# Layer 2's norm statistics and first chunk moved beside layer 1's gathers

## The chip, the core and the metric

The kernel runs on one core of a Trainium2 chip. Its engines are named as in the profile: PE (TensorE: matmuls, with PEld for its weight loads), DVE (VectorE), ACT (ScalarE), POOL (GpSimd) and SP (SyncE, here used only to issue DMA). Each engine works through its own queue in order and waits on semaphores where it needs another engine or a transfer. The metric is the device time of one execution in microseconds; the median of three runs is 15601.95 us.

## What is computed

The reference is a four-layer network on `x` of 2 x 64 x 64 x 128 (two batches of 4096 tokens with 128 channels). Cut to what matters here:

```python
# layer 1: deformable 3x3 convolution; each of 9 taps reads 4 neighbours at computed places
x = x + _L1_conv_ref(_gn(x), ...)
# layer 2, first half: norm over the channels of each token, then a selective scan
t = _to_tokens(x)
t = t + _L2_attn_ref(_ln_t(t), W_in, W_delta, W_B, W_C, W_out, A, D)

def _ln_t(v, eps=1e-5):
    return (v - mean(v, -1)) / sqrt(var(v, -1) + eps)

def _L2_attn_ref(x, ...):
    xs, z = split(x @ W_in, 2)             # 256 channels each
    delta, Bv, Cv = xs @ W_delta, xs @ W_B, xs @ W_C
    # state[d, n] = exp(delta[d] * A[d, n]) * state + delta[d] * Bv[n] * xs[d], token after token
    # y[d] = sum over n of state[d, n] * Cv[n];  out = (y * silu(z)) @ W_out
```

Layer 0 is another selective scan, layer 2's second half a spectral convolution, layer 3 a linear attention and a mixture of experts. None of these is changed.

## The kernel before

`X` holds all 8192 tokens as 64 tiles of 128 tokens by 128 channels in on-chip memory (32 KB a partition) through layers 0 and 1.

**Layer 1** (`layer1`). After some preparation it runs a loop over the 64 tiles, 32 of batch 0 and then 32 of batch 1. For a tile, POOL issues nine indirect gathers from a table in DRAM (line 598), which fill a buffer `G` of 18 KB a partition; there are four such buffers. DVE multiplies `G` by the weights of the neighbours (line 605, an operation of 4608 elements a partition). PE sums and transposes the result into `pv` (line 612), ACT copies it to `vt` (line 613), PE multiplies it by the kernel of the convolution into `po` (line 616), and DVE adds `po` to `X` (line 617). At tile 36 of the program's text stands `mix`, which prepares weights for layer 2's second half with many small DVE operations, some of ACT, and transfers on SP's queue.

**The seam.** `norm_tokens` then takes bn_stats and bn_aggr of all 64 tiles (lines 629 and 630) and computes from them `rs` (one over the standard deviation, by `rsqrt`, lines 81 to 87) and `sh` (minus mean times `rs`, line 632). `move` writes `X` to `x1` in DRAM in eight transfers (line 1410).

**Layer 2** (`layer2`) works on 16 chunks of 512 tokens. Before a chunk's scan its `prologue` is run: it reads the chunk from `x1` (line 779), normalises and transposes it (786, 787), multiplies by `w_in` (797) and, with weights that it loads one after the other (806), by `w_delta`, `w_b` and `w_c` (813, 822). What comes out is `ea` (816, 818), `drow` in DRAM (828), `g` (830) and `cv` (832). Prologues of later chunks run in steps beside the scan of the chunk before them; the first has nothing beside it, and its steps follow each other:

```python
            for _ in prologue(*todo[0], got):
                pass
            ready[0] = got.pop()
            for r in range(2):
                load_row(r)
            make_inputs(0)
```

In the scan, `load_row` (line 1127, on SP's queue) broadcasts four rows of `drow` to all partitions, `make_inputs` lets POOL multiply them by `g` into `S` (line 1139), ACT computes the decays `dA` from the row and `a_t` (line 1193), and DVE scans (line 1195). `ea` enters only from the second chunk of a batch on, `cv` only in the contraction after a group's scan.

**What sets the order.** Outside layer 2's scan the framework orders the instructions of each engine by a simulated run and places the semaphores; on the chip each engine then keeps that order. In layer 2's scan the order of the text is kept (`manual_schedule`). Pools of memory are stacked: those of layer 2 lie over those of layers 0 and 1 and over `X`, so a first write into them waits until what lay there has been read for the last time.

Of the kernel before, what the change touches and what calls it, by code (L numbers as in the profile page):

```python
# [16 lines left out]
F32 = mybir.dt.float32  # L17
# [8 lines left out]
P = 128  # L26
B, HH, WW, C = 2, 64, 64, 128
L = HH * WW
# [458 lines left out]
        nc.gpsimd.dma_start(out=dst, in_=z[: TS - 3, :])  # L487


def layer1(k, table, mix):  # L490


    tc, nc, ins, X = k.tc, k.nc, k.ins, k.X
    with ExitStack() as es:
# [97 lines left out]
        for t in range(NT):  # L592
            b, i = divmod(t, NTB)
            if t == NTB + 4 and mix is not None:
                mix(es)
            G = gp.tile([P, 9, 4 * C], F32, name="G")
            for o in range(9):
                nc.gpsimd.indirect_dma_start(  # L598
                    out=G[:, o, :],
                    out_offset=None,  # L600
                    in_=table[b],
                    in_offset=bass.IndirectOffsetOnAxis(ap=idxs[b][:, i * 9 + o : i * 9 + o + 1], axis=0),
                )
            V = G.rearrange("p o (q c) -> p (o q) c", c=C)
            nc.vector.tensor_tensor(V, V, wts[b][:, i * 9 : (i + 1) * 9, :].rearrange("p o q -> p (o q)").unsqueeze(2).to_broadcast([P, 36, C]), ALU.mult)  # L605

            vt = wk.tile([P, 9 * P], F32, name="vt")
            for g, n in ((0, 4), (4, 4), (8, 1)):
                pv = gs.tile([P, N], F32, name="pv1")
                for o in range(n):  # L610
                    for q in range(4):
                        nc.tensor.matmul(pv[:, o * P : (o + 1) * P], V[:, (g + o) * 4 + q, :], k.ident, start=q == 0, stop=q == 3)
                nc.scalar.copy(vt[:, g * P : (g + n) * P], pv[:, : n * P])  # L613
            po = po_.tile([P, C], F32, name="po2")
            for o in range(9):
                nc.tensor.matmul(po, vt[:, o * P : (o + 1) * P], w_k[:, o, :], start=o == 0, stop=o == 8)
            nc.vector.tensor_tensor(X[:, t, :], po, X[:, t, :], ALU.add)

def norm_tokens(k, rs, sh):

    tc, nc, X = k.tc, k.nc, k.X
    with tc.tile_pool(name="l2n", bufs=1) as pre:
        st = pre.tile([P, NT, 6], F32, name="st6")
        mv = pre.tile([P, NT, 2], F32, name="mv2")
        for i in range(NT):
            nc.vector.bn_stats(st[:, i, :], X[:, i, :])
            nc.vector.bn_aggr(mv[:, i, :], st[:, i, :])  # L630
        rsqrt(nc, pre, rs, mv[:, :, 1], 1e-5, [P, NT], "ln2")
        nc.vector.scalar_tensor_tensor(sh, mv[:, :, 0], -1.0, rs, ALU.mult, ALU.mult)

# [77 lines left out]
    return (wdr, mdr), work  # L714


def layer2(k, x1, x3, rs, sh, wdr, mdr):

# [18 lines left out]
    with ExitStack() as es:  # L739
# [34 lines left out]
            return x[t0 : t0 + T, :].rearrange("(i p) c -> p i c", p=P)  # L774

        def prologue(b, c, got):

            xi = sm.tile([P, NB, C], F32, name="xi", tag="s2")
            nc.sync.dma_start(out=xi, in_=chunk(x1, b, c))
            for _ in range(4):  # L780
                yield
            pt = ps.tile([P, N], F32, name="pt", tag="ps")
            for j in range(NB):
                i = b * NTB + c * NB + j
                o = sm.tile([P, C], F32, name="xn", bufs=2)
                nc.scalar.activation(o, xi[:, j, :], AF.Identity, bias=sh[:, i : i + 1], scale=rs[:, i : i + 1])
                nc.tensor.transpose(pt[:, j * P : (j + 1) * P], o, k.ident)
                yield
            xt = sm.tile([P, T], F32, name="xt2", tag="s2")
            nc.scalar.copy(xt, pt)  # L790
            xtd = ddr.tile([P, T], F32, name="xtd")
            nc.sync.dma_start(out=xtd, in_=xt)
            yield
            xs = sm.tile([P, 2, N], F32, name="xs", tag="s4")
            for h in range(2):
                px = ps.tile([P, N], F32, name="px2", tag="ps")
                nc.tensor.matmul(px, w_in[:, h * P : (h + 1) * P], xt, start=True, stop=True)
                yield
                nc.scalar.copy(xs[:, h, :], px)
            ea = cst.tile([P, 2, 256], F32, name="ea")  # L800
            g = gc.tile([P, 2, T], F32, name="g")
            cv = gc.tile([P, 2, T], F32, name="cv")
            drow = ddr.tile([256, T], F32, name="drow")
            for w_, what in (("w_delta2", 0), ("w_b2", 1), ("w_c2", 2)):
                w = cst.tile([P, 2, 256], F32, name="w")
                nc.sync.dma_start(out=w, in_=ins[w_].rearrange("(a p) c -> p a c", p=P))
                yield
                yield
                if what == 0:

                    pd = ps.tile([P, N], F32, name="pd0", tag="ps")
                    for i in range(2):
                        nc.tensor.matmul(pd[:, :256], xs[:, i, 0:1].to_broadcast([P, P]), w[:, i, :], start=i == 0, stop=i == 1)
                    yield
                    yield
                    nc.vector.tensor_tensor(ea, a_t, pd[:, :256].unsqueeze(1).to_broadcast([P, 2, 256]), ALU.mult)
                    yield
                    nc.scalar.activation(ea, ea, AF.Exp)
                for h in range(2):
                    pw = ps.tile([P, N], F32, name="pw2", tag="ps")  # L820
                    for i in range(2):
                        nc.tensor.matmul(pw, w[:, i, h * P : (h + 1) * P], xs[:, i, :], start=i == 0, stop=i == 1)  # L822
                    yield
                    yield
                    if what == 0:
                        d = sm.tile([P, N], F32, name="d", tag="s2")
                        nc.scalar.copy(d, pw)
                        nc.sync.dma_start(out=drow[h * P : (h + 1) * P, :], in_=d)
                    elif what == 1:
                        nc.vector.tensor_tensor(g[:, h, :], pw, xs[:, h, :], ALU.mult)  # L830
                    else:
                        nc.scalar.copy(cv[:, h, :], pw)
            got.append((xtd, g, cv, drow, ea))

        def epilogue(b, c, xtd, zd):

# [330 lines left out]

        with tc.manual_schedule():
            got = []
            for _ in prologue(*todo[0], got):  # L1170
                pass
            ready[0] = got.pop()
            for r in range(2):
                load_row(r)
            make_inputs(0)
# [237 lines left out]
def kernel(tc, ins, out, stages=STAGES):  # L1413
    nc = tc.nc
    with ExitStack() as es:
        pool = es.enter_context(tc.tile_pool(name="top", bufs=1))
        dr = es.enter_context(tc.tile_pool(name="topd", bufs=1, space=DRAM))
        k = Ctx(tc, ins, pool)
        x = ins["x"]
        two = "2a" in stages or "2f" in stages  # L1420
        if two:
            rs = pool.tile([P, NT], F32, name="rs2")
            sh = pool.tile([P, NT], F32, name="sh2")
        if two or "0" in stages or "1" in stages:
            with tc.tile_pool(name="x01", bufs=1) as xp:
                k.X = xp.tile([P, NT, C], F32, name="X")
                move(nc, k.X, tokens(x))
                if "1" in stages:
                    table = [dr.tile([TS * TS, 4 * C], F32, name=f"table{b}") for b in range(B)]
                    with tc.tile_pool(name="zt", bufs=1) as zp:  # L1430
                        zero_table(k, zp, table)
                mix = None
                if two:
                    weights, mix = mixing_weights(k, dr)
                if "0" in stages:
                    layer0(k)
                if "1" in stages:
                    layer1(k, table, mix)
                elif two:
                    with ExitStack() as e2:  # L1440
                        mix(e2)
                if two:
                    norm_tokens(k, rs, sh)
                x = dr.tile([B * L, C], F32, name="x1")
                move(nc, tokens(x), k.X)
        if two:
            x3 = dr.tile([B * L, C], F32, name="x3")
            layer2(k, x, x3, rs, sh, *weights)
            x = x3
        with tc.tile_pool(name="x3", bufs=1) as xp:  # L1450
            k.X = xp.tile([P, NT, C], F32, name="X")
            move(nc, k.X, tokens(x))
            if "3a" in stages:
                layer3a(k)
            if "3f" in stages:
                layer3f(k, out)
            else:
                move(nc, tokens(out), k.X)
# [106 lines left out]
```

## Time and profile before

| | us |
|---|---|
| median of 3 runs | 15601.95 |
| lowest and highest run | 15600.6, 15609.41 |
| the profiled execution's own time | 15611.47 |
| its span, first to last instruction | 15609.7 |
| first gather of layer 1 to last (line 598) | 4330.1 to 5315.2 |
| last X add of layer 1 ends (line 617) | 5338.67 |
| first S of layer 2 begins on POOL (line 1139) | 5391.72 |

Busy shares of the span are DVE 88%, POOL 86%, PE 76%, ACT 63%. Times in the profile are microseconds from the start of the span. The page lists groups of instructions as: line, engine, operation, output and inputs, count, then busy time and mean duration in ns, then the idle time of the engine before them and what ended most of it. In a timeline each row is: start, length, engine, line, operation, and in brackets the idle time before it and what released it. The chain of waits goes from the end of a window back: at each step to what released it.

### The profile page before, as it was taken

The numbers are of one execution on the slowest core, as the hardware profiler recorded it, in microseconds if no ns is written. First come the engines' busy times: TensorE is split into PE (matmuls) and PEld (weight loads), VectorE is DVE, ScalarE is ACT, GpSimd is POOL, SyncE is SP. The second block draws the span as 40 slices with busy tenths as digits, with TensorE's granted clock in tenths as the row PEclk, the third lists the DMA queues.
The fourth block names the chain that finished last, engine by engine and source line by source line (L and its number), as shares of the span: only waits on it lengthen the run. The fifth ranks groups of instructions, "written<-read, shape, count | busy, mean of one in ns | idle before, by whom it ended". The sixth has DMA issues, their size and how long they took to land.

```text
span 15609.7 us, 191436 instructions
## 1 busy us (share of the span) xinstructions
PE 11894.2 (76%) x69838; PEld 7117.6 (46%) x69838; DVE 13768.3 (88%) x12194; ACT 9829.7 (63%) x15891; POOL 13474.0 (86%) x5144
## 2 busy tenths in 40 slices
PE   6666676666677645486976978979788899898897
PEld 2222232222367512154653645646445555555565
DVE  7999979999853499999999999999999999999964
ACT  5666646666410177777777777777777777777752
POOL 6888848888578699999999999999999999999960
PEclk9999999999988767697987989989999999999998
DMA  2111111211175445465655556656666666666643
GB/s 82 71 71 70 67 60 71 73 68 71 63 226 160 137 151 163 154 195 177 204 188 169 195 179 194 202 182 200 194 193 195 192 197 202 192 196 199 188 160 130
DMA packets 1211438, 2373.47 MB, mean 152 GB/s; under 512 B 346744, under 2 KB 923896, under 8 KB 1044352
## 3 DMA queue, kind: packets, MB, share of 16 engines
q1 hardware_dynamic: 1163072, 2206.74, 43.2%
q0 software_dynamic: 46560, 153.18, 3.3%
q8 instruction: 552, 9.04, 0.2%
q14 instruction: 390, 3.19, 0.1%
q10 hardware_dynamic: 864, 1.32, 0.0%
HBM read 2018.49 MB, written 342.41 MB: 151 GB/s over the span
## 4 chain that ended last, share of the span: by engine, by line
POOL 35%; PE 14%; DVE 11%; DMA 3%; ACT 2%; issue 2%; SPq 0%; POOLq 0%; ACTq 0%; DVEq 0%
POOL S L1139 34%; DVE S L1195 10%; PE pef L1023 7%; PE Z L1157 2%; PE acc L996 2%; DMA row<-drow 2%; PE pw L822 1%; POOL S L1145 1%; ACT dA L1193 1%; ACT ze L1163 1%; DMA w<-in_w_b_dram 0%; PE acc L1058 0%; DMA e<-mdr 0%; ACT e L1003 0%; DMA w<-in_w_c_dram 0%
## 5 line engine op out<-in xcount | busy, mean ns | idle before, releaser
L1195 DVE TENSOR_TENSOR_SCAN S<-dA,S 128x512 f32<-128x512 f32 x8192 | 9226.4, 1200 | 397.2 <-ACT dA L1193 208.2
L1139 POOL TENSOR_TENSOR S<-row,g 128x4096 f32<-128x4096 f32 x1024 | 9102.2, 8895 | 280.6 <-DMA row<-drow 232.4
L1193 ACT ACTIVATE dA<-row,a_t 128x512 f32<-128x512 f32 x8192 | 5616.2, 692 | 2158.3 <-DVE S L1195 2123.3
L1157 PE MATMUL Z<-S,cv 128*32 128x256 f32 x32768 | 2504.9, 436 | 1486.0 <-ACT ze L1163 1227.3
L1023 PE MATMUL pef<-hk,ur 128*128 128x256 f32 x14336 | 3507.0, 388 | 137.8 <-ACT e L1003 122.0
L1023 PEld LDWEIGHTS pef<-hk,ur 128*128 128x128 f32 x14336 | 2642.0, 191 | 1076.6 <-issue 562.1
L376 POOL TENSOR_TENSOR S<-du,br 128x1024 f32<-128x1024 f32 x1024 | 2409.7, 2356 | 282.7 <-DVE M L401 164.9
L387 DVE TENSOR_TENSOR_SCAN S<-dA,S 128x1024 f32<-128x1024 f32 x1024 | 2338.0, 2283 | 161.2 <-ACT dA L385 101.9
L1157 PEld LDWEIGHTS Z<-S,cv 128*32 128x32 f32 x32768 | 1002.0, 121 | 2695.7 <-issue 1286.1
L419 PE MATMUL yp<-M,ident 128*128 128x512 f32 x4096 | 1974.5, 604 | 2.9 <-DVE M L401 2.9
L419 PEld LDWEIGHTS yp<-M,ident 128*128 128x128 f32 x4096 | 789.9, 193 | 2147.7 <-issue 2112.7
L385 ACT ACTIVATE dA<-dt,an 128x511 f32<-128x511 f32 x2048 | 1406.5, 687 | 194.2 <-DVE S L387 148.1
L401 DVE TENSOR_TENSOR M<-S,pcn 128x1024 f32<-128x1024 f32 x1024 | 1250.4, 1221 | 151.9 <-PE pcn L343 51.9
L343 PE MATMUL pcn<-cs,sel 80*128 80x512 bf16 x1024 | 394.7, 385 | 1183.6 <-DVE M L401 1174.7
L1163 ACT COPY ze<-Z 128x512 f32<-128x512 f32 x1024 | 1123.0, 1097 | 236.9 <-PE Z L1157 204.6
L996 PE MATMUL acc<-e,mw 128*128 128x512 f32 x1920 | 1047.6, 634 | 31.2 <-ACT e L1003 30.5
L598 POOL DMA_INDIRECT G<-table,idx x576 | 810.8, 1408 | 202.6 <-issue 170.3
L1023 PEld LDWEIGHTS pef<-hd,ur 128*128 128x128 f32 x4096 | 758.2, 194 | 491.5 <-issue 236.0
L1023 PE MATMUL pef<-hd,ur 128*128 128x256 f32 (+1 forms) x4096 | 877.8, 341 | 101.6 <-ACT e L1003 95.3
L389 ACT COPY stt<-S 128x2 f32<-128x2 f32 x896 | 169.3, 189 | 1067.9 <-DVE S L387 1064.8
L605 DVE TENSOR_TENSOR G<-G,wt 128x4608 f32<-128x4608 f32 x64 | 317.6, 4963 | 579.6 <-DMA G<-table,idx 486.4
L613 ACT COPY vt<-pv 128x512 f32<-128x512 f32 (+1 forms) x192 | 88.4, 480 | 864.9 <-remote 598.0
(331 smaller groups left out, 8503.8 us busy)
## 6 DMA issues: line engine op xcount, KB each, us to landing
row<-drow SPq DMA_DIRECT2D x1024, 1024.0 KB
br<-bc SPq DMA_DIRECT2D x256, 1024.0 KB
zd<-ze SPq DMA_DIRECT2D x1024, 256.0 KB
hk<-in_phi_dram SPq DMA_DIRECT2D x128, 576.5 KB
hk<-in_phi_dram SPq DMA_DIRECT2D x96, 704.5 KB
hd<-in_phi_dram SPq DMA_DIRECT2D x512, 128.5 KB
mw<-wdr SPq DMA_DIRECT2D x480, 128.0 KB
hk<-in_phi_dram SPq DMA_DIRECT2D x160, 320.5 KB
```

The costliest lines, as they stand in the source:

```text
L376: nc.gpsimd.tensor_tensor(S, du, br[:, n % 4, :].unsqueeze(1).to_broadcast([P, 2, T]), ALU.mult)
L385: nc.scalar.activation(dA[:, h, rest], dt[:, h, rest], AF.Exp, scale=an[:, kk * 2 + h, n : n + 1])
L387: nc.vector.tensor_tensor_scan(flat, dflat, flat, 0.0, ALU.mult, ALU.add)
L401: nc.vector.tensor_tensor(M, S, pcn.unsqueeze(1).to_broadcast([P, 2, T]), ALU.mult)
L419: nc.tensor.matmul(yp[:, h, :], k.ident, M[:, h, :], start=False, stop=n == 15)
L996: nc.tensor.matmul(acc.rearrange("p a s -> p (a s)"), ms[f][:, o, :], e, start=box["first"], stop="whole" in box and (f, o) == todo[-1])
L1023: nc.tensor.matmul(pe[:, a, 256 - n :], ur[:, par, j, :], h[:, at : at + n], start=i == 0, stop=i + 1 == len(mm))
L1139: nc.gpsimd.tensor_tensor(S, row.unsqueeze(1).to_broadcast([P, 2, R, T]), g.unsqueeze(2).to_broadcast([P, 2, R, T]), ALU.mult)
L1157: nc.tensor.matmul(Z[32 * j : 32 * j + 32, q], cv[:, h, s], S[:, h, :, s], start=h == 0, stop=h == 1)
L1163: nc.scalar.copy(ze.rearrange("p q t e -> p q e t"), Z)
L1193: nc.scalar.activation(dA, row[:, j % R, :], AF.Exp, scale=a_t[:, h, d : d + 1])
L1195: nc.vector.tensor_tensor_scan(s, dA, s, 0.0, ALU.mult, ALU.add)
```

## The change

`norm_tokens` becomes a maker of a function `each(t)`, which layer 1 calls after the X add of tile t: bn_stats and bn_aggr of this tile, after every fourth tile a transfer of four tiles to `x1`, and after the last tile of a batch the `rsqrt` and `sh` of that batch. Its small tiles lie in the pool of `X`. The body of `prologue` becomes a function `scan_inputs`, word for word. At tile 40 of the text (`t == NTB + 8`), `first_inputs` runs it for chunk 0 in layer 1, with its own loads of half of `w_in` and of `a_t`, in a pool of its own and with layer 1's PSUM tiles, and writes `g`, `cv` and `ea` to DRAM. Layer 2 reads these three back by transfers on ACT's queue where it ran the first prologue.

```diff
@@ layer1
             if t == NTB + 4 and mix is not None:
                 mix(es)
+            if t == NTB + 8 and first is not None:
+                first(es, ps)
...
             nc.vector.tensor_tensor(X[:, t, :], po, X[:, t, :], ALU.add)
+            if each is not None:
+                each(t)

-def norm_tokens(k, rs, sh):
-    tc, nc, X = k.tc, k.nc, k.X
-    with tc.tile_pool(name="l2n", bufs=1) as pre:
...
-        for i in range(NT):
-            nc.vector.bn_stats(st[:, i, :], X[:, i, :])
-            nc.vector.bn_aggr(mv[:, i, :], st[:, i, :])
-        rsqrt(nc, pre, rs, mv[:, :, 1], 1e-5, [P, NT], "ln2")
-        nc.vector.scalar_tensor_tensor(sh, mv[:, :, 0], -1.0, rs, ALU.mult, ALU.mult)
+def norm_tokens(k, pool, x1, rs, sh):
...
+    def each(t):
+        nc.vector.bn_stats(st[:, t, :], X[:, t, :])
+        nc.vector.bn_aggr(mv[:, t, :], st[:, t, :])
+        if t % 4 == 3:
+            nc.sync.dma_start(out=out[:, t - 3 : t + 1, :], in_=X[:, t - 3 : t + 1, :])
+        if t % NTB == NTB - 1:
+            b = slice(t + 1 - NTB, t + 1)
+            rsqrt(nc, pool, rs[:, b], mv[:, b, 1], 1e-5, [P, NTB], "ln2")
+            nc.vector.scalar_tensor_tensor(sh[:, b], mv[:, b, 0], -1.0, rs[:, b], ALU.mult, ALU.mult)
+    return each

+def first_inputs(k, es, ps, dr, x1, rs, sh):
+    nc = k.nc
+    pool = es.enter_context(k.tc.tile_pool(name="l2e", bufs=1))
+    w_in = pool.tile([P, 256], F32, name="w_in0")
+    nc.sync.dma_start(out=w_in, in_=k.ins["w_in2"][:, :256])
+    a_t = pool.tile([P, 2, 256], F32, name="a_t0")
+    nc.sync.dma_start(out=a_t, in_=k.ins["a2"].rearrange("(a p) c -> p a c", p=P))
+    got = []
+    for _ in scan_inputs(k, 0, 0, x1, rs, sh, w_in, a_t, pool, pool, pool, dr, ps, got):
+        pass
+    xtd, g, cv, drow, ea = got[0]
+    kept = []
+    for t, name in ((g, "g0"), (cv, "cv0"), (ea, "ea0")):
+        d = dr.tile(list(t.shape), F32, name=name)
+        nc.sync.dma_start(out=d, in_=t)
+        kept.append(d)
+    return xtd, kept[0], kept[1], drow, kept[2]

@@ layer2
             got = []
-            for _ in prologue(*todo[0], got):
-                pass
-            ready[0] = got.pop()
+            xtd, g0, cv0, drow, ea0 = early
+            g, cv, ea = gc.tile([P, 2, T], F32, name="g"), gc.tile([P, 2, T], F32, name="cv"), cst.tile([P, 2, 256], F32, name="ea")
+            for dst, src in ((g, g0), (cv, cv0), (ea, ea0)):
+                nc.scalar.dma_start(out=dst, in_=src)
+            ready[0] = xtd, g, cv, drow, ea
             for r in range(2):
                 load_row(r)
             make_inputs(0)

@@ tile_hybrid_kernel
-                    layer1(k, table, mix)
+                    x1, early = dr.tile([B * L, C], F32, name="x1"), []
+                    each = norm_tokens(k, xp, x1, rs, sh)
+                    first = lambda es, ps: early.append(first_inputs(k, es, ps, dr, x1, rs, sh))
+                    layer1(k, table, mix, each, first)
...
-                    norm_tokens(k, rs, sh)
-                x = dr.tile([B * L, C], F32, name="x1")
-                move(nc, tokens(x), k.X)
...
-            layer2(k, x, x3, rs, sh, *weights)
+            layer2(k, x, x3, rs, sh, *weights, early[0])
```

More of the change, by code (lines that the diff above doesn't have):

```diff
@@ L487, in zero_table, with layer1 @@
         nc.gpsimd.dma_start(out=dst, in_=z[: TS - 3, :])
-def layer1(k, table, mix):
+def layer1(k, table, mix, each, first):
     tc, nc, ins, X = k.tc, k.nc, k.ins, k.X
@@ L617, in layer1 @@
             nc.vector.tensor_tensor(X[:, t, :], po, X[:, t, :], ALU.add)
-def norm_tokens(k, rs, sh):
-    tc, nc, X = k.tc, k.nc, k.X
-    with tc.tile_pool(name="l2n", bufs=1) as pre:
-        st = pre.tile([P, NT, 6], F32, name="st6")
-        mv = pre.tile([P, NT, 2], F32, name="mv2")
-        for i in range(NT):
-            nc.vector.bn_stats(st[:, i, :], X[:, i, :])
-            nc.vector.bn_aggr(mv[:, i, :], st[:, i, :])
-        rsqrt(nc, pre, rs, mv[:, :, 1], 1e-5, [P, NT], "ln2")
-        nc.vector.scalar_tensor_tensor(sh, mv[:, :, 0], -1.0, rs, ALU.mult, ALU.mult)
+            if each is not None:
+                each(t)
+def norm_tokens(k, pool, x1, rs, sh):
+    nc, X = k.nc, k.X
+    st = pool.tile([P, NT, 6], F32, name="st6")
+    mv = pool.tile([P, NT, 2], F32, name="mv2")
+    out = x1.rearrange("(i p) c -> p i c", p=P)
+    def each(t):
[8 more added lines that the diff above has]
+    return each
 DW = 257
@@ L714, in mixing_weights, with scan_inputs @@
     return (wdr, mdr), work
-def layer2(k, x1, x3, rs, sh, wdr, mdr):
+def scan_inputs(k, b, c, x1, rs, sh, w_in, a_t, sm, cst, gc, ddr, ps, got):
+    nc, ins, T = k.nc, k.ins, N
+    NB = T // P
+    xi = sm.tile([P, NB, C], F32, name="xi", tag="s2")
+    nc.sync.dma_start(out=xi, in_=x1[b * L + c * T : b * L + (c + 1) * T, :].rearrange("(i p) c -> p i c", p=P))
+    for _ in range(4):
+        yield
+    pt = ps.tile([P, N], F32, name="pt", tag="ps")
+    for j in range(NB):
+        i = b * NTB + c * NB + j
+        o = sm.tile([P, C], F32, name="xn", bufs=2)
+        nc.scalar.activation(o, xi[:, j, :], AF.Identity, bias=sh[:, i : i + 1], scale=rs[:, i : i + 1])
+        nc.tensor.transpose(pt[:, j * P : (j + 1) * P], o, k.ident)
+        yield
+    xt = sm.tile([P, T], F32, name="xt2", tag="s2")
+    nc.scalar.copy(xt, pt)
+    xtd = ddr.tile([P, T], F32, name="xtd")
+    nc.sync.dma_start(out=xtd, in_=xt)
+    yield
+    xs = sm.tile([P, 2, N], F32, name="xs", tag="s4")
+    for h in range(2):
+        px = ps.tile([P, N], F32, name="px2", tag="ps")
+        nc.tensor.matmul(px, w_in[:, h * P : (h + 1) * P], xt, start=True, stop=True)
+        yield
+        nc.scalar.copy(xs[:, h, :], px)
+    ea = cst.tile([P, 2, 256], F32, name="ea")
+    g = gc.tile([P, 2, T], F32, name="g")
+    cv = gc.tile([P, 2, T], F32, name="cv")
+    drow = ddr.tile([256, T], F32, name="drow")
+    for w_, what in (("w_delta2", 0), ("w_b2", 1), ("w_c2", 2)):
+        w = cst.tile([P, 2, 256], F32, name="w")
+        nc.sync.dma_start(out=w, in_=ins[w_].rearrange("(a p) c -> p a c", p=P))
+        yield
+        yield
+        if what == 0:
+            pd = ps.tile([P, N], F32, name="pd0", tag="ps")
+            for i in range(2):
+                nc.tensor.matmul(pd[:, :256], xs[:, i, 0:1].to_broadcast([P, P]), w[:, i, :], start=i == 0, stop=i == 1)
+            yield
+            yield
+            nc.vector.tensor_tensor(ea, a_t, pd[:, :256].unsqueeze(1).to_broadcast([P, 2, 256]), ALU.mult)
+            yield
+            nc.scalar.activation(ea, ea, AF.Exp)
+        for h in range(2):
+            pw = ps.tile([P, N], F32, name="pw2", tag="ps")
+            for i in range(2):
+                nc.tensor.matmul(pw, w[:, i, h * P : (h + 1) * P], xs[:, i, :], start=i == 0, stop=i == 1)
+            yield
+            yield
+            if what == 0:
+                d = sm.tile([P, N], F32, name="d", tag="s2")
+                nc.scalar.copy(d, pw)
+                nc.sync.dma_start(out=drow[h * P : (h + 1) * P, :], in_=d)
+            elif what == 1:
+                nc.vector.tensor_tensor(g[:, h, :], pw, xs[:, h, :], ALU.mult)
+            else:
+                nc.scalar.copy(cv[:, h, :], pw)
+    got.append((xtd, g, cv, drow, ea))
@@ L731, in layer2 @@
+def layer2(k, x1, x3, rs, sh, wdr, mdr, early):
     tc, nc, ins = k.tc, k.nc, k.ins
@@ L776, in prologue @@
         def prologue(b, c, got):
[L778 to L832, printed above, removed]
@@ L833, in prologue @@
-            got.append((xtd, g, cv, drow, ea))
+            return scan_inputs(k, b, c, x1, rs, sh, w_in, a_t, sm, cst, gc, ddr, ps, got)
         def epilogue(b, c, xtd, zd):
@@ L1436 @@
                     layer0(k)
+                each = first = None
+                if two:
+                    x1, early = dr.tile([B * L, C], F32, name="x1"), []
+                    each = norm_tokens(k, xp, x1, rs, sh)
+                    first = lambda es, ps: early.append(first_inputs(k, es, ps, dr, x1, rs, sh))
                 if "1" in stages:
-                    layer1(k, table, mix)
+                    layer1(k, table, mix, each, first)
                 elif two:
@@ L1441 @@
                         mix(e2)
+                        for t in range(NT):
+                            each(t)
+                        first(e2, e2.enter_context(tc.tile_pool(name="l2ep", bufs=2, space=PSUM)))
                 if two:
-                    norm_tokens(k, rs, sh)
-                x = dr.tile([B * L, C], F32, name="x1")
-                move(nc, tokens(x), k.X)
+                    x = x1
+                else:
+                    x = dr.tile([B * L, C], F32, name="x1")
+                    move(nc, tokens(x), k.X)
         if two:
             x3 = dr.tile([B * L, C], F32, name="x3")
-            layer2(k, x, x3, rs, sh, *weights)
+            layer2(k, x, x3, rs, sh, *weights, early[0])
             x = x3
```

## The prediction

> **What bounds the kernel now.** I read the page first, then the chain of waits around the seam between layers 1 and 2, then the timelines of POOL, DVE, ACT and SP inside layer 1's gather loop. The scan of layer 2, two thirds of the span, keeps POOL and DVE near 90% busy, and the change leaves its code alone. What it touches is the seam, and the loop into which the seam's work goes. The chain of waits from 5290 to 5420 us (start, length, what):
>
> ```profile
> 5315.19 3.67 DMA G<-table,idx
> 5319.17 4.96 DVE G L605
> ...
> 5338.38 0.29 DVE X L617
> 5338.67 0.39 DVE st L629 x2
> ...
> 5355.33 0.21 DVE ln_v L81
> ...
> 5357.50 0.23 DVE sh L632
> 5357.76 0.50 ACT xn L786
> ...
> 5386.22 4.90 DMA row<-drow
> 5391.72 8.82 POOL S L1139
> 5400.57 7.58 DVE S L1195 x7
> ```
>
> Layer 1 ends with the last X add at 5338.67. POOL's first S, which starts the scan, begins at 5391.72, so the seam is 53.05 us long and serial: 64 pairs of statistics (to 5355.33, 16.7), the rsqrt and shift (to 5357.76, 2.4), the first chunk's preparation (to 5386.22, 28.5) and the row broadcast (5.5).
>
> The loop is bound by POOL. The page:
>
> ```profile
> L598 POOL DMA_INDIRECT G<-table,idx x576 | 810.8, 1408 | 202.6 <-issue 170.3
> ```
>
> 810.8 busy plus 170.3 of issue fills 981 of the 986 us from 4330 to 5315: the next gather is always ready to go. The timelines of POOL and DVE for one tile:
>
> ```profile
> 4695.29 4.96 DVE L605 TENSOR_TENSOR G<-G,wt 128x4608 f32<-128x4608 f32 x1 [9.94 <-DMA G<-table,idx]
> 4700.16 0.28 DVE L617 TENSOR_TENSOR X<-po,X 128x128 f32<-128x128 f32 x1
> ```
> ```profile
> 4695.01 0.95 POOL L598 DMA_INDIRECT G<-table,idx  x1 [0.30 <-issue]
> 4696.26 4.80 POOL L598 DMA_INDIRECT G<-table,idx  x1 [0.30 <-issue]
> 4701.37 0.95 POOL L598 DMA_INDIRECT G<-table,idx  x1 [0.31 <-issue]
> ```
>
> A gather takes 0.95 + 0.30, but the one that begins under the product L605 takes 4.80 and ends 0.81 after it. A tile is thus 8 x 1.25 + 5.1 = 15.1 us, of which DVE's long two-input product costs POOL 3.85. DVE itself then idles about 10 us a tile; PE is busy 798.7 of 1010 us, so it has about 3.2 us a tile to spare. The question of this case is whether work put into that idle time stays free for POOL.
>
> **Part 1, the statistics tile by tile.** It takes 16.7 off the seam's path and adds to each tile one bn_stats (0.26) and one bn_aggr (0.17), chained 0.26 a pair. In DVE's 10 idle us they cost DVE nothing. What they cost POOL the trace does not show. Lower bound 0: the X add, the nearest row in place, reads one operand from PSUM and one from SBUF and starts right behind the product; the gather still ends 0.81 after the product (4701.06), where a gather that had to wait for the add (4700.44) too would end later. Upper bound from the small DVE operations of the weight mixing at 4442.7 to 4447.1: the three gathers beside them took 1.15, 1.02 and 1.55, together 0.87 over 0.95 each, or 0.2 us per us of DVE work; 64 x 0.43 x 0.2 = 5.5. Full blocking, 64 x 0.43 = 27.5, is the far bound. I take 0, since the new operations read one SBUF operand like the add. The two rsqrts (eight small instructions each) together cost POOL under 1.
>
> The Trainium skill, "SBUF — State Buffer", section "Who interferes with whom", calls the pair of ports that DVE shares with GpSimd an exclusive lock: the loser is blocked for the whole instruction. If the new operations held it, that rule alone would charge 27.5. The same section says that a one-input operation outside the two-port modes does not contend, which charges 0; and it holds that a tensor_tensor should not stall descriptor generation, which the 4.80 row contradicts.
>
> **Part 2, the first chunk inside batch 1's gathers.** It takes 28.5 off the path. It adds about 24 us of PE (4 transposes 1.4, px 4.2, pd 2.1, six pw pairs 16.1), about 6 of ACT, 2 of DVE, no POOL instruction, and on SP's queue some 12 transfers, beside only the x1 stores, for which nothing in the loop waits. PE's spare 3.2 us a tile takes 24 us in eight tiles, and 23 tiles remain behind its place. What could show is delay: gather t+4 needs PE to be done with G of tile t. L605 of tile t starts at 4695.29 and PE ends with that tile at 4715.0; the gathers of t+4 start three periods after those of t+1 (4692.5), at 4737.8, so PE may be 22.8 us late before POOL notices. A precedent, timelines of ACT and PE:
>
> ```profile
> 4428.06 0.20 ACT L663 ACTIVATE y<-y 128x4 f32<-128x4 f32 x1 [9.76 <-DVE iv L684]
> ```
> ```profile
> 4431.07 2.50 PE L616 MATMUL po<-w_k,vt 128*128 128x128 f32 x10 [8.95 <-ACT vt L613]
> ```
>
> There a small ACT operation waited 9.76 for DVE, the vt copies queued behind it waited too, PE stalled 8.95, and POOL ran on with 0.30 gaps. The new steps do this more often: the Sqrt at batch 0's end waits for a DVE step that stands behind a later product, and DVE's queue holds the first X add (4402.10) behind the fourth product (4395.46), so ACT and PE may be held until DVE is up to three tiles ahead. Cost: 0 if all of it fits into 22.8; 15 if the chain (28.5) and one such hold (9) come together, 28.5 + 9 - 22.8. I take 4, nearer the precedent's 0. The transfers are some 4 MB; no gather waits for them.
>
> **Part 3, what the seam then waits for.** Left are the last tile's statistics, the broadcast, and three reads back (g, cv, ea) on ACT's queue. The SP timeline shows when memory comes free:
>
> ```profile
> 5336.36 0.36 SPq L779 DMA_DIRECT2D xi<-x  x1
> 5338.70 0.36 SPq L1410 DMA_DIRECT2D x<-X  x1
> 5357.80 0.35 SPq L758 DMA_DIRECT2D w_in<-in_w_in_dram  x1
> ```
>
> xi went out when PE had read the last G (pv, 5328.29 to 5336.33 in the chain), ahead of the last x1 store; w_in lies where X lay and waited for the shift. If the row loads go like xi, POOL's S can begin 5.50 after 5336.36 (5386.22 to 5391.72), at 5341.9. g needs layer 1's constants free, at 5338.4; bounded by the weight load of L806 (256 KB, 2.83 in the chain) and the row (1 MB, 5.50), it lands 5341.6 to 5344. Three rows and g share the engines, so I take 5344.5: gain 47. If the rows stand behind w_in, which waits for the last shift (5338.67 + 0.43 + 2.4 = 5341.5), then three issues (1.3) and 5.5 give 5348.3: gain 43.4. I take 46, nearer the first since SP showed that order. cv, ea and a_t are needed only when S ends, 8.8 later.
>
> Sum: 46 - 4 = 42. The profiled execution took 15611.5 (span 15609.7), near the top of the runs (15600.6 to 15609.4); I subtract from their median, 15601.95: 15560, or -0.27%.
>
> **Rivals.** A difference within 0.2%, 31 us, is what a measurement of this kernel can hardly tell from none.
> - *The gain is given back in the loop.* The statistics block gathers in full (27.5), or PE falls behind by 10 to 25 more and POOL waits for G. For it: POOL has no slack and L605 does block it. Against it: the X add and the precedent above. Gain 46 - 27.5 - 4 = 14.5, so 15587; with PE's lag alone 15566 to 15581, mostly no change. 0.21.
> - *Slower: DVE's queue is put in another order.* If a tile's X add and statistics stand ahead of the next tile's product, instead of three products later, each tile becomes a chain: product 4.96, pv 8.04, po 2.02, add 0.29, pair 0.43, handoffs 0.5 = 16.2, and 18.6 where pv takes 10.4 as at 4704.57 to 4715.0. It decides once this passes 15.1: 63 x 1.1 = 70 to 63 x 3.5 = 220 lost, against 46 gained: 15626 to 15776. Against it: nothing in the data needs that order. 0.09 with other losses.
> - *The seam shrinks less*: every load waits until X is free. That is the 43.4 case, 15563, inside the forecast.
>
> **How the numbers follow.** The forecast, faster by over 31, has 0.70, "no change" 0.21, slower 0.09. Low end: the earliest S (5341.9, gain 49.8), no loop cost, and 5 for the spread of the runs: 15547. High end: the full-blocking case, 15588. The slower case and some of the tails stay outside.
>
> **What would show it.** Right: bn_stats between products with neighbouring gathers still 0.95 and periods of 15.1; POOL's idle time still only issue; first S 3 to 10 us after the last X add; no L786 behind that add. Wrong: L598's mean above 1408 ns; POOL waiting for PE pv; gathers ending over 0.81 after the product; an SP order with the rows behind w_in, or ACT's g issue later than 5339.

## The result and the profile after

The changed kernel took 15569.74 us on the median of 16 runs (15559.30 to 15582.81), the kernel before 15602.28 beside it (16 runs, 15590.98 to 15613.76). The ratio is 0.9979, with a 95% interval of 0.9973 to 0.9986: 32.5 us or 0.21% faster. The forecast was 15560, the range 15547 to 15588.

The chain of waits of the changed kernel at the seam (start, length, what):

```profile
5356.68 0.30 DVE X L619
5357.00 5.13 DMA x<-X
5362.24 0.04 issue
5362.28 0.34 SPq L851
...
5363.66 6.81 DMA row<-drow
...
5370.70 7.49 DVE S L1234 x7
```

The last X add ends at 5356.98 and DVE's first scan starts at 5370.70; POOL's first S starts at 5361.73. From X add to S it is now 4.75 us, where it was 53.05. What is left in this chain is the last store of `X` and the broadcast of a row. The timelines of SP, ACT and POOL show in which order the transfers went:

```profile
5354.66 0.33 SPq L1164 DMA_DIRECT2D row<-drow  x1
5356.68 0.35 ACTq L1210 DMA_DIRECT2D g<-g  x1
5357.00 0.36 SPq L638 DMA_DIRECT2D x<-X  x1
5357.41 0.50 SPq L1164 DMA_DIRECT2D row<-drow  x1
5361.73 35.26 POOL L1176 TENSOR_TENSOR S<-row,g 128x4096 f32<-128x4096 f32 x4 [27.37 <-DMA x<-X]
5362.28 0.34 SPq L851 DMA_DIRECT2D w_in<-in_w_in_dram  x1
```

The first row load goes 2.3 us ahead of the X add's end, and `w_in` behind the first two rows. The read back of `g` is issued by ACT at 5356.68, when the last `po` is done; it takes 4.6 us to land, and S starts 5.05 after the issue. The profile puts S's wait down to the last store of `X` to `x1`, issued 0.32 later. The two end so close together that the trace does not show which of them decides.

The loop is the other half. The page's group of gathers, and from the view of that line what POOL waited for:

```profile
L600 POOL DMA_INDIRECT G<-table,idx x576 | 813.9, 1413 | 216.6 <-issue 167.3
```
```profile
L600 POOL DMA_INDIRECT G<-table,idx x576: 942/946/5731, 4331.3 to 5333.4; - x192
...
  PE pv L614: 14.2, 1
```

The mean gather is 1413 ns against 1408: 3.1 us of busy time over all 576, which lies within the scatter of the profiles below (1401 to 1416 with the product unchanged). But POOL stood still once, for 14.2 us, until PE had read a buffer `G`; in the kernel before, all such waits were 0.3. From first to last gather it takes 1002.1 us instead of 985.1. The seam gave 48.3, the loop took back 17.0, and from the first gather to the first S it is 1030.4 us instead of 1061.6: 31.2 less, next to the 32.5 of the medians.

The timelines of the engines ahead of that wait (start, length, engine, line, operation; in brackets the idle time before and what ended it):

```profile
5005.28 4.96 DVE L607 TENSOR_TENSOR G<-G,wt 128x4608 f32<-128x4608 f32 x1 [7.57 <-DMA G<-table,idx]
5010.15 0.28 DVE L619 TENSOR_TENSOR X<-po,X 128x128 f32<-128x128 f32 x1
5010.47 0.36 SPq L638 DMA_DIRECT2D x<-X  x1
5010.90 0.66 DVE L770 TENSOR_TENSOR ea<-a_t,pd 128x512 f32<-128x512 f32 x1
5010.92 0.46 SPq L760 DMA_DIRECT2D w<-in_w_b_dram  x1
5011.59 0.63 ACT L772 ACTIVATE ea<-ea 128x512 f32<-128x512 f32 x1 [21.64 <-DVE ea L770]
5015.36 5.14 PE L776 MATMUL pw<-xs,w 128*128 128x512 f32 x8 [20.29 <-DMA w<-in_w_b_dram]
5027.23 1.28 DVE L784 TENSOR_TENSOR g<-pw,xs 128x512 f32<-128x512 f32 x2
5027.97 3.23 PE L776 MATMUL pw<-xs,w 128*128 128x512 f32 x4 [2.65 <-DVE g L784]
5032.80 0.95 POOL L600 DMA_INDIRECT G<-table,idx  x1 [14.24 <-PE pv L614]
```

To be read from the top: a product of a later tile starts on DVE as soon as its gathers have landed. Behind it in DVE's queue stands an X add, and behind that the chunk's `ea`. SP's next entry is the store of that X to `x1`, so SP waits for the X add, and the load of `w_b` waits behind the store, though PE was done with `w_delta` in that buffer at 4992.4. ACT's next entry is the Exp of `ea`, so ACT stands still for 21.64, and with it the copies `vt` queued behind it. PE's next entry needs `w_b`; it stands still for 20.29, with the `pv` of two tiles queued behind. A second hold follows: the next `pw` needs a PSUM tile (a buffer for the results of matmuls) that DVE's `g` has still to read, and `g` stands behind the next product (to 5027.2).

### The profile page after: what moved, and what is told of

Its sections match the earlier page's. It is cut to its first block, busy times and chain, and to the rows that moved or that the text cites. A ratio compares the mean times of both kernels' runs of the same rounds, so it can differ in the third digit from the quotient of the medians.

```text
span 15569.5 us, 191480 instructions
## 1 busy us (share of the span) xinstructions
PE 11851.7 (76%) x69838; PEld 7103.6 (46%) x69838; DVE 13786.1 (89%) x12201; ACT 9836.6 (63%) x15894; POOL 13475.7 (87%) x5144
## 4 chain that ended last, share of the span: by engine, by line
POOL 35%; PE 13%; DVE 11%; DMA 3%; issue 2%; ACT 2%; SPq 0%; POOLq 0%; ACTq 0%; DVEq 0%
POOL S L1176 34%; DVE S L1234 10%; PE pef L1060 6%; PE Z L1194 2%; PE acc L1033 2%; DMA row<-drow 2%; PE pw L776 1%; POOL S L1182 1%; ACT ze L1200 1%; ACT dA L1232 0%; DMA w<-in_w_b_dram 0%; PE acc L1095 0%; SPq L883 0%; ACT e L1040 0%; DMA e<-mdr 0%
## 5 line engine op out<-in xcount | busy, mean ns | idle before, releaser
L600 POOL DMA_INDIRECT G<-table,idx x576 | 813.9, 1413 | 216.6 <-issue 167.3
L1040 ACT COPY e<-pef 128x512 f32<-128x512 f32 x960 | 557.8, 587 | 109.8 <-PE pef L1060 61.0
```

## The experiments

**Theory.** The 14.2 us are several holds of in-order queues (SP's store ahead of a load, ACT's Exp, PE's PSUM tile), each of which waits for a DVE step behind a later tile's product. **Rivals.** SP's queue alone; ACT's `ea` step alone; the chunk's work is too much for PE wherever it is put; or the statistics on DVE slow POOL.

All kernels in one table, in us. From first gather to first S is the loop, then the last tile (22 to 27 us, in e6 36), then the seam. Times behind the first S scatter by themselves: from first S to the span's end the profiles show 10,201 to 10,226 us with no order in it, so the columns of the front part tell apart what medians of runs cannot. They come from one profile a row; where one kernel was profiled twice, the loop differs by 3.2 and 3.3 us and POOL's wait by 1.7 and 0.9. e2 to e5 ran once each, so only their traces count. e1 to e4 were measured together, then e5 to e8, then e9 to e12.

| kernel | first to last gather | POOL's wait for PE `pv` | X add to first S | first gather to first S | median (runs) |
|---|---|---|---|---|---|
| before | 985.1 | 0.3 | 53.05 | 1061.6 | 15602.28 (16) |
| after | 1002.1 | 14.2 | 4.75 | 1030.4 | 15569.74 (16) |
| after, again (e11) | 998.8 | 12.5 | 4.5 | 1026.8 | 15570.91 (11) |
| e1 statistics only | 989.7 | 0.3 | 39.1 | 1050.8 | 15592.36 (10) |
| e5 statistics x4 | 981.4 | none | 39.4 | 1044.5 | 15582.06 (1) |
| e2 `w` in 3 buffers | 1004.6 | 19.3 | 5.3 | 1033.8 | 15570.10 (1) |
| e3 no `ea` step | 996.7 | 13.0 | 4.7 | 1023.8 | 15578.84 (1) |
| e4 e2 and e3 | 999.6 | 18.5 | 4.9 | 1029.6 | 15576.52 (1) |
| e7 no holds | 985.0 | 2.1 | 4.9 | 1015.5 | 15557.74 (9) |
| e8 spread | 985.9 | none | 4.5 | 1015.4 | 15564.67 (11) |
| spread, again (e12) | 989.1 | 0.9 | 5.0 | 1019.5 | 15555.80 (7) |
| e6 e7, weights in PSUM | 930.1 | 211.9 | 5.8 | 972.2 | 15526.26 (5) |
| e9 spread, weights in PSUM | 740.1 | 6.3 | 5.1 | 772.1 | 15324.86 (5) |
| e10 before, weights in PSUM | 735.3 | 3.4 | 55.3 | 812.7 | 15348.15 (5) |

In e3, e4, e6 and e7 the early chunk's `ea` is not computed (two matmuls, a DVE step of 0.66 us, an Exp); the scan does not use it for the first chunk.

**e1, the statistics alone.** The first chunk's preparation goes back into layer 2:

```diff
-            xtd, g0, cv0, drow, ea0 = early
...
+            for _ in prologue(*todo[0], got):
+                pass
+            ready[0] = got.pop()
```

> Part 1 alone: statistics tile by tile, the first chunk's preparation back in layer 2. Theory (holds): the loop's cost in the changed kernel, 17 us, is one wait of 14.2 us for PE and 3 us in the gathers; without the preparation in the loop the wait is gone, the last gather starts near 5319 (5315.2 before, 5333.4 after), and the statistics cost POOL about 3. The seam, from the last X add to the first S, is then 33 to 37 us (2.9 for the last rsqrt, up to 28.5 for the preparation, 5.5 for the row): about 12 us faster than before, 15590. Rival (statistics block the gathers): the last gather starts near 5330 here too, and the time is no better than before.

The seam is 39.1, 14 less than before but 2 over the expected 33 to 37, and POOL has no wait for PE over 0.3. Beside the run of before on its chip (15599.89) the ratio is 0.9997, interval 0.9987 to 1.0007: no difference that the runs can tell. In the profile the front part is 10.8 shorter. So part 1 is worth some 10 us, and the wait comes with part 2.

**e5, the statistics four times.** e1, with bn_stats and bn_aggr of every tile repeated:

```diff
+        for _ in range(4):
             nc.vector.bn_stats(st[:, t, :], X[:, t, :])
             nc.vector.bn_aggr(mv[:, t, :], st[:, t, :])
```

> The statistics alone beside the gathers (the first chunk's preparation at its old place), with bn_stats and bn_aggr of each tile done four times over. Theory (they lie beside the gathers and cost nothing that can be told apart): first to last gather 985 to 1,000 us, against 990 with them once. Rival (each blocks POOL's descriptors for its time, as the product does, about 0.43 us a tile): 83 us more, about 1,070 us, and the time near 15,670.

981.4 from first to last gather, no more than with the statistics once (989.7) or in layer 2 (985.1). The mean gather is 1401 ns:

```profile
L600 POOL DMA_INDIRECT G<-table,idx x576 | 807.2, 1401 | 202.6 <-issue 157.2
```

The rival of a block falls, by a factor: some 90 us more of these operations (292 and 179 ns each here, 192 more pairs) cost nothing that stands out of a scatter of a few us. The 4.6 us that the loop of e1 is longer than before's is not their price either.

**e2, `w` in three buffers** in the early chunk, so that its loads need not wait for a free buffer:

```diff
-        w = cst.tile([P, 2, 256], F32, name="w")
+        w = cst.tile([P, 2, 256], F32, name="w", bufs=wb)   # 3 in the early chunk
```

> The three weight matrices of the early chunk get a buffer each, so SP loads them long before and no load stands behind an x1 store. Theory (several holds, each of them enough): ACT's Exp and PE's last product with w_c still wait for DVE operations that stand behind a later product L607, so PE is still held until that product and POOL still waits 8 to 14 us for G (14.2 after). Rival (SP's queue alone): the wait falls to 0 to 2. Rival (24 us of work on PE are too much): the wait stays at 14.

No shorter: 19.3. PE is let go by another releaser, at the same place of the program (timelines of ACT and PE):

```profile
5012.88 0.63 ACT L772 ACTIVATE ea<-ea 128x512 f32<-128x512 f32 x1 [20.57 <-DVE ea L770]
5012.90 5.78 PE L776 MATMUL pw<-xs,w 128*128 128x512 f32 x8 [18.13 <-DVE ea L770]
5029.06 3.78 PE L776 MATMUL pw<-xs,w 128*128 128x512 f32 x4 [7.77 <-DVE g L784]
```

With the loads out of the way, `ea` releases PE 6.3 us after the product's start (5006.57) instead of 10.1, and then the hold by `g` is 7.77 instead of 2.65. SP's queue alone is not the cause; my 8 to 14 was too low.

**e3, no `ea` step in the early chunk** (pd, the multiply and the Exp left out).

> The early chunk leaves out ea (pd, DVE's product, Exp), which the first chunk of a batch does not use. Theory (several holds): w_b's load still stands behind an x1 store on SP, so POOL's wait stays at 10 to 14. Rival (ACT held by DVE's ea alone): 0 to 3.

13.0, as expected: ACT's step alone is not the cause.

**e4, both.**

> Early weights and no ea together. Theory (several holds): one hold is left, the product g on DVE, which stands behind the next L607 and keeps the PSUM tile that PE's last product of the early chunk needs; POOL's wait for PE stays at 8 to 14. Rival (SP's queue and ea are all of it): 0 to 2, last gather near 5319, time 15555.

18.5, against an expectation of 8 to 14. Two holds remained, one of them not on my list (timelines of SP, ACT and PE for that one):

```profile
5004.08 0.36 SPq L638 DMA_DIRECT2D x<-X  x1
5004.53 5.00 SPq L782 DMA_DIRECT2D drow<-d  x2
5008.59 0.58 ACT L781 COPY d<-pw 128x512 f32<-128x512 f32 x1 [25.78 <-DMA drow<-d]
5009.23 3.78 PE L776 MATMUL pw<-xs,w 128*128 128x512 f32 x4 [21.89 <-ACT d L781]
```

`d` has one buffer, so its second copy waits until the first is stored to `drow`; that store stands on SP behind an `x1` store, which waits for an X add behind a product. ACT waits 25.78 for it and PE 21.89 for ACT. The other is the `g` hold (7.15). In the changed kernel the hold by `d` lay hidden under the others: there ACT's second copy waited 3.58 for `drow` (to 5016.76), when the load of `w_b` had already let PE go (5015.36).

**e7, all holds taken away.** e4, with two buffers for `d` and a copy of the matmul's result by ACT ahead of the multiply, so that PE's PSUM tiles come free without DVE:

```diff
-                d = sm.tile([P, N], F32, name="d", tag="s2")
+                d = sm.tile([P, N], F32, name="d0", bufs=2)
...
-                nc.vector.tensor_tensor(g[:, h, :], pw, xs[:, h, :], ALU.mult)
+                bv = sm.tile([P, N], F32, name="bv", bufs=2)
+                nc.scalar.copy(bv, pw)
+                nc.vector.tensor_tensor(g[:, h, :], bv, xs[:, h, :], ALU.mult)
```

> The fourth of the version before it (w in three buffers, no decay step in the early chunk) and the two holds left there taken away: d has two buffers of its own, and ScalarE copies the product's matmul result out of PSUM so that TensorE does not wait for VectorE's multiply. All of the chunk's matmuls then stand together behind one tile. Theory (several holds, each enough alone): with all of them gone POOL waits 0 to 3 us for TensorE, last gather 985 to 990 us after the first, S about 5 us after the last X add, about 15,555 on the median. Rival (some 24 us of TensorE work in one place are too much by themselves): POOL still waits 10 us or more.

2.1 us of waits, 985.0 from first to last gather, 15557.74. PE's timeline shows the whole chunk in one place:

```profile
5000.80 1.93 PE L751 MATMUL px<-xt,w_in 128*128 128x512 f32 x4
5002.56 10.55 PE L776 MATMUL pw<-xs,w 128*128 128x512 f32 x24
5012.94 6.41 PE L614 MATMUL pv<-ident,G 128*128 128x128 f32 x56
```

All six pairs of `pw` take 10.55 us without a gap, and POOL hardly notices. The rival "too much work for PE" falls; what counted was that PE stood still, not that it worked. The work is also smaller than I had it: px and pw 12.5 here, where I took 4.2 + 16.1 from the seam. The matmuls themselves are shorter: a record of `pw` takes 596 ns on the mean here and one of `px` 604, at a granted clock of 1.00 (5000 to 5013); in the seam of the kernel before they took 846 and 1141, at a mean granted clock of 0.69 (5357 to 5387).

**e8, the chunk spread over tiles.** The same work and buffers as in the changed kernel; `first_inputs` now stops at each `yield`, and two of its steps follow each tile (the rest of the edit only passes the generator on):

```diff
+            if t >= NTB + 8 and first is not None:
+                for _ in range(2):
+                    next(steps, None)
```

> Same work as after; the first chunk's preparation is handed out over some 20 tiles of batch 1, two of its steps behind each tile, instead of all behind one tile. The weights keep their one buffer, the decay step stays. Theory (the 14.2 us for which POOL waited are the chunk's steps queued behind steps of later tiles; TensorE has about 2.5 us to spare in each tile, so one step a tile goes in beside the gathers): waits of POOL for TensorE 0 to 4 us, last gather 988 to 993 us after the first, S 4 to 6 us after the last X add, some 10 to 14 us less than after, so 15,555 to 15,560 on the median. Rival (the chunk's work on the engines is simply too much beside the gathers, wherever it is put): the last gather stays 1,000 us or more behind the first and the time at about 15,570.

POOL has no wait for PE left, and the loop is that of the kernel before, 985.9. One pair of `pw` now goes in behind a tile's `po` (timelines of PE and POOL):

```profile
5112.20 2.17 PE L621 MATMUL po<-w_k,vt 128*128 128x128 f32 x18
5113.72 0.95 POOL L603 DMA_INDIRECT G<-table,idx  x1 [0.30 <-issue]
5114.21 1.88 PE L779 MATMUL pw<-xs,w 128*128 128x512 f32 x4
5115.93 7.31 PE L617 MATMUL pv<-ident,G 128*128 128x128 f32 x64
```

`w` and `d` still have one buffer and `ea` is computed: a hold of the same kind still comes (ACT's second copy into `d` waited 5.91 for `drow`), but it has a whole tile in which to be made up. The front part is 15.0 us shorter than the change's. The median of 15564.67 lies above the 15,555 to 15,560 that were expected and shows only 5 of these 15.

**e11 and e12, the change and the spread version once more,** on one chip.

> The changed kernel as it is, beside the others on one chip. POOL's single wait for TensorE between 10 and 20 us again, first S near 5,360, 15,560 to 15,580 on the median.

> The version that hands the first chunk out over some 20 tiles, once more beside the unaltered change. No wait of POOL for TensorE over 1 us, first S near 5,347, and 8 to 15 us less than the unaltered change beside it on the median.

Waits of 12.5 against 0.9, front parts 1026.8 against 1019.5, medians 15570.91 against 15555.80. To the kernel before, the ratios are 0.9980 (0.9971 to 0.9989) and 0.9971 (0.9960 to 0.9982). The order is that of the traces both times, but the intervals overlap: the loss in the loop is shown by the waits, not by the medians.

**e6, the product with one SBUF input.** SBUF is the on-chip memory that holds `X`, `G` and the weights. e7, with the tile's 36 weights copied by DVE into PSUM (the code is shortened). To make room, the pool of PSUM tiles for layer 1's preparation and the early chunk goes from three to two; the tiles of `pv`, which take what comes from `G`, keep their three, other than the expectation says:

```diff
+            wp = wp_.tile([P, 36], F32, name="wp")            # PSUM
+            nc.vector.tensor_copy(wp, wts[b][...])
-            nc.vector.tensor_tensor(V, V, wts[b][...].to_broadcast([P, 36, C]), ALU.mult)
+            nc.vector.tensor_tensor(V, V, wp.unsqueeze(2).to_broadcast([P, 36, C]), ALU.mult)
```

> The version without holds, and the 36 neighbour weights of each tile are copied by VectorE into PSUM, so that the product over the gathered tile has one SBUF input instead of two (PSUM buffers of the gather results 3 to 2 for the room). Theory (a gather is slow, 4.8 us instead of 0.95, because VectorE's product with two SBUF inputs stands beside it): those gathers fall to about 0.95, the tile's period from about 15.1 to 12.5 us where TensorE becomes the bound, and the time by up to 160 us, to about 15,390 to 15,450. Rival (the slow gather has another cause, such as waiting for the buffer): gathers stay at 4.8 and the time at 15,550 to 15,575.

The gathers fall to 961 ns in the mean, so the cause was right. The time did not follow, 15526 instead of 15,390 to 15,450: in this profile PE sets the period, 13.3 to 13.9 us a tile near 4800, although its 90 records need 10.4 when they run without gaps. **e9** does the same to e8, **e10** to the kernel before.

> The changed kernel with the first chunk handed out over some 20 tiles, and the product's 36 weights of each tile in PSUM (decay step kept, weights in one buffer). Theory (with the gathers at 0.95 us TensorE sets the tile's period, 13.4 us where the product with PSUM weights was looked at): last gather 925 to 940 us after the first, first S near 5,300 to 5,310, and 15,520 to 15,535 on the median. Rival (the chunk's TensorE work, now spread over tiles that TensorE bounds, shows in full there): the loop is 20 us or more longer than 930 us and the time over 15,545.

> The kernel before, with only the product's 36 weights of each tile in PSUM; statistics and first chunk stay in layer 2. Theory (a gather waits while VectorE works from two SBUF inputs; TensorE is the bound once that is gone): tile period about 13.2 us, loop from first to last gather 905 to 930 us instead of 985, and 15,525 to 15,550 on the median; against the run with the first chunk spread it shows what the change still brings when TensorE bounds the loop: 46 less the chunk's 24 us of TensorE work, so about 20 us. Rival (the change keeps its whole gain): 40 us or more slower than that run.

Both missed their numbers by 180 to 210 us, on the fast side. The pages' groups of gathers of e9 and e6:

```profile
L604 POOL DMA_INDIRECT G<-table,idx x576 | 561.0, 974 | 207.2 <-issue 191.5
```
```profile
L601 POOL DMA_INDIRECT G<-table,idx x576 | 553.7, 961 | 404.3 <-PE pv L617 211.9
```

And the timelines of DVE and POOL in e9, with a product and the two gathers under it:

```profile
4807.48 4.96 DVE L613 TENSOR_TENSOR G<-G,wp 128x4608 f32<-128x4608 f32 x1 [5.99 <-DMA G<-table,idx]
4807.51 0.94 POOL L604 DMA_INDIRECT G<-table,idx  x1 [0.30 <-issue]
4808.76 0.95 POOL L604 DMA_INDIRECT G<-table,idx  x1 [0.30 <-issue]
```

A gather under the product takes 0.95 instead of 4.80; the product itself stays at 4.96. In e9 and e10 the loop is bound by POOL, at 11.3 us a tile (nine times 0.95 + 0.30), and PE just keeps up: it is busy for 675 of 741 us in e9, and POOL waits 6.3 and 3.4 us for it. So the theory that PE sets the period fell; my 13.4 us a tile was taken from e6. What the move still brings here is not settled: from first gather to first S, e9 is 40.6 shorter than e10, as the rival said, but by the medians of five runs each only 23.3, where the theory had about 20. e9 beats the kernel before by 1.76% (ratio 0.9824, 0.9810 to 0.9837); nearly all of that is the weights' place, not the change.

## Why the prediction was right, and where not

The time lay in the range, 10 us above the forecast; the direction was right, by 32.5 against the bound of 31 that was set for telling it from no change. That this bound was passed is luck: in e11, the same change beside the kernel before once more, the difference of the medians is 28.25. And what happened in the loop is what the first rival describes: PE falls behind and POOL waits for `G`. 15569.74 lies in the 15566 to 15581 that it gave for that. Of the signs that were set for being wrong, POOL's wait for PE `pv` came; the mean gather of 1413, over the 1408 named there, is within the scatter.

- *The seam.* Forecast 46 (43.4 to 49.8), measured 48.3. The order on SP was the one taken: rows ahead of `w_in`. S started 0.4 us after `g` had landed, as said, though the last store of `X` ended at about the same time.
- *Part 1 on POOL.* Forecast 0, far bound 27.5. e1 and e5 bear it out: repeated four times, the statistics still cost nothing. The Trainium skill, "SBUF — State Buffer", section "Who interferes with whom", says that a VectorE instruction with at most one SBUF input outside the two-port modes does not contend with GpSimd; e5 agrees for bn_stats and bn_aggr, and so does the product of e9.
- *Part 2 in the loop: this is the step that failed.* Forecast 4, with 15 as its upper end; the wait was 14.2 and 12.5 in two profiles, the loop 17.0 and 13.7 longer. The prediction had the mechanism (ACT and PE held by DVE steps behind later products, a margin of 22.8) and the upper end, but leaned to the precedent's 0. Its sentence that SP's transfers lie beside only the `x1` stores, "for which nothing in the loop waits", was wrong: nothing waits for the stores, but the stores wait for an X add, and the load of `w_b`, for which PE waits, is queued behind one. And the precedent was one hold of 9; here a hold of 20 was followed by the chunk's own work and, in the first profile, a second hold.
- *The size of PE's work* was too high (24; with the chunk in one piece, px and pw take 12.5 instead of 20.3), since it was taken from the serial seam, where the granted clock was 0.69 instead of 1.00. This error and the one on the holds worked against each other, so that the upper end of 15 comes so near to 14.2 is luck too.
- *The sum.* 46 - 4 = 42 was forecast; 48.3 - 17.0 = 31.3 came. Of the 17.0, 14.2 turned into a new wait, and the remaining 3 are no more than the scatter; e7 and e8 get the wait back in the traces (front parts 46 shorter than before's; 42 in e12).

## What to carry to other kernels

Work moved into the idle time of several engines must be followed queue by queue: an entry that is off every critical path, such as a store, still holds the entries behind it until its own producer is done. Hand such work out in steps as small as what one period has to spare; spread over tiles, most holds could be left in place, where in one piece every remainder of them that was tried still stalled the loop. And look first at the operation that sets the loop's period: here a copy of 36 weights per tile into PSUM was worth 251 us (e10), nearly eight times what the move brought.

## What the runs showed of the hardware

- An indirect gather issued by POOL takes 0.95 us beside the X adds and the statistics, but mostly 4.6 to 5.7 when it begins under the multiply with two SBUF inputs; with one of these in PSUM it is 0.95 again, under a multiply of the same 4.96 us. While `mix` runs, some gathers take longer with either multiply (1.0 to 2.0 us in e10). The same section of the skill says that a VectorE instruction with two SBUF inputs contends with a GpSimd instruction that reads SBUF, which fits the 4.80; but it also infers that a tensor_tensor, which takes only the read side of the shared ports, does not stall descriptor generation, and there the runs say otherwise for a gather whose indices lie in SBUF.
- In some profiles PE worked in bursts: some matmuls of a tile ran in small groups (one to six of them in e6 near 4800, at a granted clock of mostly 1.00), with idle times of 0.2 to 1.7 us that the profile puts down to "issue". For `pv` this idle time is 112.2 us in e6, 40.6, 21.7 and 27.2 in e5, e7 and e8, which were measured together with e6, and 57.6 in the kernel before; the changed kernel, e1 to e4 and e9 to e12 have none in the loop. e8 and e12 are the same kernel (views of their `pv` line on PE, with what ended its idle time):

```profile
L617 PE MATMUL pv<-ident,G x4608: 269/275/423, 4357.9 to 5339.9; 128*128 128x128 f32 x192
...
  issue: 27.2, 48
```
```profile
L617 PE MATMUL pv<-ident,G x4608: 272/275/582, 4355.7 to 5342.7; 128*128 128x128 f32 x192
...
  DVE G L610: 9.0, 1
```

So the kernel alone does not decide it. Where POOL sets the period it costs nothing that can be seen (loops of 985.9 and 989.1); in e6 it came with a loop of 930.1 where e9 has 740.1. e6 was measured only beside e5, e7 and e8, and e9 and e10 only in the later group, so whether e6's own program or the conditions of that group made it slow is not shown. The cause is open; e6 was not run again.
